# Four graph-attention layers on one core: layer 3's features turned through DRAM, layer 1's unit kept one higher, adj's turned copy in three places

## The chip, the cores and the metric

The kernel runs on one core of one Trainium2 chip. The metric is device time in microseconds (us), as the median of several executions. One further execution was taken with the hardware profiler; its views are what is read here. The engines are TensorE (PE in the profile, its weight loads PEld), VectorE (DVE), ScalarE (ACT), GpSimd (POOL) and SyncE (SP), which issues nearly all DMAs.

## The reference

128 graphs of 128 nodes with 512 float32 features go through four layers. Each layer normalises its input, applies relu and adds the result of an attention to the input. `adj` is an integer matrix per graph that says which nodes may attend to which.

```python
for layer in (L0, L1, L2, L3):
    x = x + layer(maximum(layernorm(x), 0))
# L1: two GAT layers; the first with 4 heads of 256 features
h = elu(gat_layer(x, mask, W1, ..., b1, concat=True))     # 1024 features
h = gat_layer(h, mask, W2, ..., b2, concat=False)         # 512 features
# L3: 8 heads of 64 features
xp = x @ W_proj;  out = relu(softmax(mask(leaky_relu(src_i + dst_j + b))) @ xp)
```

Layer 1's mask is indexed the other way round from the others (its softmax runs over the other axis), which is why the kernel holds `adj` turned as well.

## The kernel before, in words

One graph is one tile `xt` of 128 nodes x 512 features; everything of a graph stays in SBUF but for a few exchanges through DRAM. Up to 16 graphs are in flight (`FLYING`, line 22).

**Who sets the order.** The kernel is written as generators that yield single steps (`Step`, an instruction, or `Group`, several on one engine), requests for a tile (`Take`), or waits for another stream. A `Scheduler` (its `issue`, `rank`, `plan`) runs all of them against a small table of costs (`Step.estimate`) when the program is built, and so writes one fixed order for each engine. On the chip each engine takes its instructions strictly in that order and waits by semaphores. All steps are called from one line of `issue`, so that the profile puts nearly everything on line 331 (332 in the changed kernel); the tiles' names tell the steps apart. `plan` sets due times from one rehearsed graph, stretched over `FLYING` graphs.

**Tiles.** Kinds of tiles share pools of places: "mid" tiles (`h`, `ht`, `t`, `e1`, `et1`, `x2`, `x3`) have 18 together, "big" and "small" 10 and 22, each kind with a limit of its own. `adj` and its turned copy `at_t` have six places each (`FLYING // 4 + 2`, four graphs a tile).

**A layer.** `norm_relu` takes statistics on VectorE, three small steps on GpSimd and a relu on ScalarE (`h`). Where a layer multiplies features by a weight (layers 1 and 3), `transposed` turns `h` first: four 128x128 transposes on TensorE against `ident` into a PSUM bank, and a ScalarE copy to `ht`. `projected` multiplies `ht` with the weight: `w1x` in three parts of 344 columns for layer 1, `wpx` in two parts of 264 for layer 3. In the profile each float32 matmul stands as two records.

**Turning through DRAM.** VectorE's transpose turns squares of 32x32 in place; it doesn't move a square to another group of partitions. `exchanged` does the rest: four DMAs write a tile to DRAM square by square and one reads it back with rows and columns of squares exchanged. Layer 1's attention weights (512 columns, `et1`) and layer 3's (1024 columns, `et3`) are turned in this manner, layers 0, 1 and 2 use `dealt_out` for a single 128x128 tile. The last five graphs (`late`, `LATE = 5`) turn on TensorE instead, and the first eight in layer 0, the first three in layer 1.

**Layer 1's unit** (in `layer1`, after the first attention): per half of the 1024 features, VectorE adds `b1` to the PSUM bank into `y`, clamps `y` at 0 from above into `t`, ScalarE takes `exp(t)`, and VectorE makes `max(t - 1, y)`. `projected` then multiplies `y` with `w2x` (two parts of 257 columns, eight matmuls each) and VectorE adds `b2`. The weights' extra two columns of `w2x` are made once in `fold_w2`.

**adj turned.** `load_turned` reads four graphs of `adj` with squares exchanged, and VectorE turns the squares in place once per four graphs; `layer1`'s mask is made from it.

Of the kernel before, what the change touches and what calls it, by code (L numbers as in the profile page):

```python
# [9 lines left out]
F32 = mybir.dt.float32  # L10
I32 = mybir.dt.int32
# [7 lines left out]
LOWEST = -3.0e38  # L19
SLOPE = 0.2  # L20
EPS = 1e-5
FLYING = 16
PATIENCE = .3
LANES = 8
AHEAD = 1
# [4 lines left out]
SLOW = 0.7  # L30
FIRST = 0.8
MARGIN = .6
BIG, MID, SMALL = 10, 18, 22
SHARED = {k: ("big", BIG) for k in ("xl", "y1", "e3", "et3")}
SHARED.update({k: ("small", SMALL) for k in ("m0", "m1", "m2", "m3", "row", "e0", "et0")})
SHARED.update({k: ("mid", MID) for k in ("h", "ht", "t", "e1", "et1", "x2", "x3")})

# [90 lines left out]
class Take:  # L130


    def __init__(self, pool, shape, kind, most):
        self.pool, self.shape, self.kind, self.most = pool, shape, kind, most
        self.tag, self.bufs = SHARED.get(kind, (kind, most))


# [34 lines left out]
class Scheduler:  # L172
# [61 lines left out]
    def take(self, want):  # L234

        _, free = heapq.heappop(self.returned[want.tag])
        t = want.pool.tile(want.shape, F32, tag=want.tag, name=want.kind, bufs=want.bufs)
        self.tag_of[t.tensor.name] = want.tag, want.kind
        self.held[want.kind] = self.held.get(want.kind, 0) + 1
        return t, free  # L240
# [119 lines left out]
def kernel(  # L360
# [64 lines left out]
    products = const.tile([P, D], F32, name="products")  # L425
    minus_half = const.tile([P, 1], F32, name="minus_half")
    nc.gpsimd.memset(minus_half, -0.5)

# [26 lines left out]
    def few(to, values):  # L457
        with nc.allow_non_contiguous_dma(reason="at most 1024 values, once"):
            nc.scalar.dma_start(out=to, in_=values)

    def setup():
        for i, a in enumerate((l0_a1, l0_a2)):
            few(a0[:, :, i], a.rearrange("(c p) o -> p (c o)", p=P))
        for i, a in enumerate((l1_src1, l1_dst1)):
            few(a1[:, :, i], a.rearrange("h (c p) -> p (h c)", p=P))
        few(b1, l1_b1.rearrange("(c p) -> p c", p=P))

        w0 = []
        for c in range(KC):
            if c % 2 == 0:  # L470
                pair = yield tile_of("e3", 4, H3 * P)
                pair = pair.rearrange("p (c f) -> p c f", c=2)
            w0.append(pair[:, c % 2])
            yield S.dma_start(out=w0[c], in_=l0_w[c * P : (c + 1) * P])
        yield Fork(fold_u(w0))
        yield from load(0)
        yield from load_turned(0)
        for c in range(KC):
            yield S.dma_start(out=w1x[c][:, E1:], in_=l1_w1[c * P : (c + 1) * P])
        yield Fork(fold_w1())  # L480
        yield Fork(setup_second(), SECOND)

    def setup_second():
        yield from load(1)
        yield from load(2)
        vecs = []
        for row in (l1_src2, l1_dst2):
            vecs.append((yield tile_of("x2", 3, E2 + D))[:, :D])
            yield S.dma_start(out=vecs[-1], in_=row[0].partition_broadcast(P))
        for c in range(FC):  # L490
            yield S.dma_start(out=w2x[c][:, E2:], in_=l1_w2[c * P : (c + 1) * P])
        yield Fork(fold_w2(vecs), FOLD2)
        yield S.dma_start(out=b2[:, E2:], in_=l1_b2.partition_broadcast(P))
        yield Fork(setup_third(), THIRD)

    def setup_third():
# [64 lines left out]
    def fold_w2(vecs):  # L561
        for w in w2x:
            for s, vec in enumerate(vecs):
                yield from dot(w[:, E2:], vec, w[:, s : s + 1])
        give_back(*vecs)
        sched.reached.add("w2")

    def fold_w3(wa):
# [12 lines left out]
        sched.reached.add("wp")  # L581


    def norm_relu(xt):

        n = nc.vector.BN_STATS_DIM
        st = yield tile_of("st", 6, n + 5)
        yield V.bn_stats(st[:, :n], xt)
        mean, var = st[:, n : n + 1], st[:, n + 1 : n + 2]
        yield V.bn_aggr(st[:, n : n + 2], st[:, :n])  # L590
        ve, rstd, nmr = (st[:, i : i + 1] for i in range(n + 2, n + 5))
        yield G.tensor_scalar(ve, var, EPS, None, ALU.add)
        yield G.tensor_tensor(out=rstd, in0=ve, in1=minus_half, op=ALU.pow)
        yield G.tensor_scalar(nmr, mean, rstd, -1.0, ALU.mult, ALU.mult)
        h = yield tile_of("h", 5, D)
        yield A.activation(out=h, in_=xt, func=AF.Relu, bias=nmr, scale=rstd)
        give_back(st)
        return h

    def dot(h, vec, to):  # L600

        yield V.tensor_tensor_reduce(
            out=products,
            in0=h,
            in1=vec,
            scale=1.0,
            scalar=0.0,
            op0=ALU.mult,
            op1=ALU.add,
            accum_out=to,  # L610
        )

    def blocks_of(t):

# [223 lines left out]
    def layer1(xt, mask, late, near):  # L838
# [43 lines left out]
        for g in range(0, FC, 4):  # L882
            po = yield bank()
            yield Group(
                [
                    T.matmul(
                        po[:, (c - g) * P : (c - g + 1) * P],
                        lhsT=xl[:, c * P : (c + 1) * P],
                        rhs=et[c * P // F1],
                        start=True,  # L890
                        stop=True,
                    )
                    for c in range(g, g + 4)
                ]
            )
            if g + 4 == FC:
                give_back(fx, et[0])
            yg = y[:, g : g + 4, :]
            yield V.tensor_tensor(
                yg,  # L900
                po.rearrange("p (j q) -> p j q", q=P),
                b1[:, g : g + 4].unsqueeze(2).to_broadcast([P, 4, P]),
                ALU.add,
            )
            give_back(po)

            yg = yg.rearrange("p c q -> p (c q)")
            t = yield tile_of("t", 5, 4 * P)
            yield V.tensor_scalar(t, yg, 0.0, None, ALU.min)
            yield A.activation(out=t, in_=t, func=AF.Exp)  # L910
            yield V.scalar_tensor_tensor(yg, t, -1.0, yg, ALU.add, ALU.max)
            give_back(t)
        yield Until("w2")
        gx = yield tile_of("x2", 3, E2 + D)
# [19 lines left out]

    def layer3(xt, mask, late):

        h = yield from norm_relu(xt)
        ht = yield from transposed(blocks_of(h), "ht", 4)
        give_back(h)
        yield Until("wp")  # L940

        fx = yield tile_of("x3", 4, H3, E3 + K3 + 1)
# [102 lines left out]
    def load(b):  # L1045

        xs[b] = xpool.tile([P, D], F32, tag="xt", name="xt")
        yield S.dma_start(out=xs[b], in_=x[b])
        if b % AG == 0:
            adjs[b // AG] = adjp.tile([P, AG, P], I32, tag="at", name="at")  # L1050
            yield S.dma_start(
                out=adjs[b // AG], in_=adj[b : b + AG].rearrange("g i j -> i g j")
            )
            if b >= FLYING + AHEAD:
                yield Fork(load_turned(b))
            elif b:
                yield from load_turned(b)
        sched.reached.add(("x", b))

    def load_turned(b):  # L1060

        adjs_t[b // AG] = t = adjp.tile([P, AG, P], I32, tag="at_t", name="at_t")
        yield Group(
            [
                S.dma_start(
                    out=t[m * Q : (m + 1) * Q].rearrange("b g (r c) -> b (g r) c", r=R),
                    in_=adj[b : b + AG, :, m * Q : (m + 1) * Q].rearrange(
                        "g (r b) c -> b (g r) c", r=R
                    ),
                )  # L1070
                for m in range(R)
            ]
        )
        sched.reached.add(("loaded", b // AG))
# [6 lines left out]
    def graph(b):  # L1081
# [12 lines left out]
            yield V.transpose(flat, flat)  # L1094
            sched.reached.add(("turned", b // AG))
        yield Until(("turned", b // AG))
        at = adjs_t[b // AG][:, b % AG, :]
        m1 = yield tile_of("m1", 8, P)
        yield V.scalar_tensor_tensor(m1, at, 0.0, neg_off_diag, ALU.is_le, ALU.mult)
        yield from layer1(xt, m1, late, b < NEAR)  # L1100
        give_back(m1)
        m2 = yield tile_of("m2", 5, P)
# [5 lines left out]
        yield from layer3(xt, m3, late)  # L1108
        yield S.dma_start(out=out[b], in_=xt)

    adjs, adjs_t, xs = {}, {}, {}
    with tc.manual_schedule():
        usual = EARLY if EARLY % AG == 0 and EARLY < B - LATE else 0
        sched.rehearse(load(usual))
        sched.rehearse(load_turned(usual))
        sched.plan(sched.rehearse(graph(usual)))
        sched.reached.clear()
        sched.add(setup(), 0)
        flying, started = [], 0
        while True:  # L1120
            flying = [s for s in flying if not s.over]
            if started < B and len(flying) < FLYING:
                flying.append(sched.add(graph(started), started, "graph"))
                started += 1
            if not sched.issue() and started == B:
                break
# [49 lines left out]
```

## Time and profile before

| what | value |
|---|---|
| median of 3 runs | 3185.19 us (3175.77 to 3188.9) |
| profiled execution, its own time | 3175.9 us |
| its span, first to last instruction | 3174.1 us, 64620 instructions |
| mean granted TensorE clock | 0.993 |
| DMA: bytes, share of 16 engines (SP's queue) | 456.53 MB, 56.0% |
| DMAs that SP issues | 3614 |
| TensorE, records of `wpx,ht` | 2048, 505.1 us busy |
| TensorE, records of `w2x,y` | 4096, 967.5 us busy |
| VectorE, `y<-t,y` 128x512 | 256, 173.3 us busy, 677 ns each |
| ScalarE, `t<-t` 128x512 | 256, 160.4 us busy, 626 ns each |
| ScalarE, `h<-xt,st` 128x512 | 512, 412.2 us busy, 808 ns each |

How it is read: a group's line gives line, engine and operation, `out<-in` by the program's names, shapes, xcount, then busy time of the whole group, mean ns of one, and the idle time of the engine before its instructions with what ended most of it. A busy time is a union of spans, so overlapped instructions count once there but in full in the mean. The timeline gives start, duration, engine, operation and count, neighbours merged. The waits add up for each engine who released it. In the chain of waits, each piece is what the last instruction was waiting for, followed back to the start.

### The profile page before, as it was taken

The numbers are of one execution on the slowest core, as the hardware profiler recorded it, in microseconds if no ns is written. First come the engines' busy times: TensorE is split into PE (matmuls) and PEld (weight loads), VectorE is DVE, ScalarE is ACT, GpSimd is POOL, SyncE is SP. The second block draws the span as 40 slices with busy tenths as digits, with TensorE's granted clock in tenths as the row PEclk, the third lists the DMA queues.
The fourth block names the chain that finished last, engine by engine and source line by source line (L and its number), as shares of the span: only waits on it lengthen the run. The fifth ranks groups of instructions, "written<-read, shape, count | busy, mean of one in ns | idle before, by whom it ended". The sixth has DMA issues, their size and how long they took to land.

```text
span 3174.1 us, 64620 instructions
## 1 busy us (share of the span) xinstructions
PE 3133.4 (99%) x17434; PEld 2391.5 (75%) x17434; DVE 2869.5 (90%) x11663; ACT 2458.1 (77%) x7224; POOL 934.8 (29%) x2313
## 2 busy tenths in 40 slices
PE   8999999999999999999999999999999999999997
PEld 5777777777777777777777777777777777777786
DVE  6989989999999999999999999999999999899886
ACT  5777778778777877777787787778778777877867
POOL 2222222233232323323322332332323233233222
PEclk8999999999999999999999999999999999999998
DMA  7245565656565555555565556566565556555442
GB/s 193 53 96 144 152 155 150 150 148 160 147 154 153 153 148 156 155 146 154 147 160 148 153 159 149 146 154 152 153 158 151 147 155 161 145 147 147 114 112 82
DMA packets 770101, 460.68 MB, mean 145 GB/s; under 512 B 344776, under 2 KB 702408, under 8 KB 769736
## 3 DMA queue, kind: packets, MB, share of 16 engines
q1 hardware_dynamic: 765560, 456.53, 56.0%
q8 instruction: 140, 2.29, 0.3%
q14 instruction: 225, 1.84, 0.2%
q10 hardware_dynamic: 4176, 0.02, 0.1%
HBM read 299.00 MB, written 157.33 MB: 144 GB/s over the span
## 4 chain that ended last, share of the span: by engine, by line
PE 84%; DVE 6%; DMA 5%; ACT 2%; issue 1%; SPq 1%; POOL 1%; ACTq 0%; DVEq 0%; POOLq 0%
PE bank L331 84%; DVE e L331 2%; DMA et<-exchanged 1%; DMA row<-d 1%; DMA d<-r 1%; DVE st L331 1%; DMA et<-dealt 1%; DVE xt L331 1%; DVE products L331 1%; ACT e L331 1%; SPq L331 1%; DVE t L331 1%; POOL st L331 1%; DVE y L331 0%; DVE c L331 0%
## 5 line engine op out<-in xcount | busy, mean ns | idle before, releaser
L331 PE MATMUL bank<-w2x,y 128*128 128x257 f32 x4096 | 967.5, 381 | 0.0
L331 PE MATMUL bank<-w1x,ht 128*128 128x344 f32 x3072 | 951.6, 453 | 2.6 <-ACT ht L331 2.6
L331 PEld LDWEIGHTS bank<-w2x,y 128*128 128x128 f32 x4096 | 759.1, 190 | 138.6 <-issue 25.4
L331 PEld LDWEIGHTS bank<-w1x,ht 128*128 128x128 f32 x3072 | 573.3, 190 | 282.9 <-issue 27.3
L331 ACT ACTIVATE e<-e,f 128x128 f32<-128x128 f32 x2176 | 752.1, 391 | 8.4 <-DVE c L331 7.6
L331 POOL TENSOR_SCALAR st<-st 128x1 f32<-128x1 f32 x1024 | 343.5, 336 | 1174.6 <-DVE st L331 773.1
L331 ACT ACTIVATE e<-e,c 128x128 f32<-128x128 f32 x1408 | 535.4, 394 | 124.9 <-DVE e L331 78.5
L331 PE MATMUL bank<-wpx,ht 128*128 128x264 f32 x2048 | 505.1, 390 | 0.2 <-ACT ht L331 0.2
L331 ACT ACTIVATE h<-xt,st 128x512 f32<-128x512 f32 x512 | 412.2, 808 | 66.1 <-POOL st L331 61.6
L331 PEld LDWEIGHTS bank<-wpx,ht 128*128 128x128 f32 x2048 | 379.2, 191 | 81.0 <-issue 14.9
L331 POOL TENSOR_TENSOR st<-st,minus_half 128x1 f32<-128x1 f32 x512 | 353.8, 692 | 37.4 <-POOL st L331 0.2
L331 DVE BATCH_NORM_STATS2 st<-xt 128x6 f32<-128x512 f32 x512 | 346.4, 678 | 0.0
L331 DVE CUSTOM_DVE_ANT_0 e<-e,m 128x128 f32<-128x128 f32 x1484 | 334.4, 284 | 13.2 <-DMA e<-d 13.0
L331 PEld LDWEIGHTS bank<-et,xl 128*128 128x128 f32 x2048 | 267.1, 191 | 46.6 <-issue 16.9
L331 ACT COPY xl<-bank 128x344 f32<-128x344 f32 x384 | 168.0, 439 | 138.8 <-PE bank L331 134.7
L331 PE MATMUL bank<-h,et 128*128 128x512 f32 x512 | 265.8, 601 | 7.0 <-DMA et<-dealt 4.3
L331 PE MATMUL bank<-et,xl 128*128 128x128 f32 x2048 | 270.2, 275 | 1.6 <-DMA et<-exchanged 1.5
L331 DVE SCALAR_TENSOR_TENSOR xt<-bank,c,xt 128x512 f32<-128x512 f32 x256 | 190.6, 747 | 58.9 <-PE bank L331 55.4
L331 ACT ACTIVATE t<-t 128x512 f32<-128x512 f32 x256 | 160.4, 626 | 84.6 <-DVE t L331 83.0
L331 DVE TENSOR_TENSOR y<-bank,b 128x512 f32<-128x512 f32 x256 | 173.8, 679 | 24.1 <-PE bank L331 22.4
L331 ACT COPY ht<-bank 128x512 f32<-128x512 f32 x274 | 158.6, 580 | 38.0 <-PE bank L331 35.1
L331 DVE STREAM_TRANSPOSE e<-e 128x128 f32<-128x128 f32 (+1 forms) x481 | 187.8, 392 | 0.0
(85 smaller groups left out, 4220.2 us busy)
## 6 DMA issues: line engine op xcount, KB each, us to landing
e<-d SPq DMA_DIRECT2D x123, 512.0 KB
exchanged<-e SPq DMA_DIRECT2D x492, 128.0 KB
et<-exchanged SPq DMA_DIRECT2D x123, 512.0 KB
xt<-in_x_dram SPq DMA_DIRECT2D x128, 256.0 KB
out_dram<-xt SPq DMA_DIRECT2D x128, 256.0 KB
e<-d SPq DMA_DIRECT2D x125, 256.0 KB
exchanged<-e SPq DMA_DIRECT2D x480, 64.0 KB
et<-exchanged SPq DMA_DIRECT2D x120, 256.0 KB
```

The lines of the kernel that those rows point to most:

```text
L331: method(*args, **kw)
```

## The change

- **Layer 3** (all graphs but the last five): `norm_relu` writes `h` with its 32-column squares in another order (`dealt=True`), `exchanged` sends it through DRAM into a new "mid" tile `hs`, and one VectorE transpose of 128x512 turns the squares back into `h`, whose four blocks of 128 columns then take the place of `ht`. TensorE's four transposes and ScalarE's copy are gone there.
- **Layer 1**: `b1` is made one higher once, so that `y` holds the value plus 1; ScalarE takes `exp(y - 1)` straight from `y`, VectorE makes `max(min(t, 1), y)`. So `y` is the unit plus 1, without the clamp. `fold_w2` makes up for it: GpSimd sums the eight tiles of `w2x`, two matmuls with a tile of ones add that over the partitions, and VectorE subtracts it from `b2`.
- **adj**: `at_t` has three places, asked for from the scheduler and given back after the mask of the fourth graph; its load is a stream of its own from the 13th graph on.
- `FLYING` goes from 16 to 17, "mid" from 18 to 20 places, `h` may hold 6 of them (5 before).

```diff
-FLYING = 16
+FLYING = 17
...
-BIG, MID, SMALL = 10, 18, 22
+BIG, MID, SMALL = 10, 20, 22
+TURNED = 3
...
+        yield G.tensor_scalar(b1, b1, 1.0, None, ALU.add)
...
+        total = yield tile_of("x2", 3, E2 + D)
+        yield G.tensor_tensor(total, w2x[0], w2x[1], ALU.add)
+        for w in w2x[2:]:
+            yield G.tensor_tensor(total, total, w, ALU.add)
+        for to, part in zip(columns(b2, 2), columns(total, 2)):
+            pm = yield bank()
+            pm = pm[:, : to.shape[1]]
+            yield T.matmul(pm, lhsT=one.to_broadcast([P, P]), rhs=part, start=True, stop=True)
+            yield V.tensor_tensor(to, to, pm, ALU.subtract)
+            give_back(pm)
+        give_back(total)
...
-        h = yield tile_of("h", 5, D)
-        yield A.activation(out=h, in_=xt, func=AF.Relu, bias=nmr, scale=rstd)
+        h = yield tile_of("h", 6, D)
+        to, of = h, xt
+        if dealt:
+            to = h.rearrange("p (m c b) -> p c m b", c=KC, b=Q)
+            of = xt.rearrange("p (c m b) -> p c m b", c=KC, b=Q)
+        yield A.activation(out=to, in_=of, func=AF.Relu, bias=nmr, scale=rstd)
...
+    def features_turned(xt, turned_here):
+
+        if turned_here:
+            h = yield from norm_relu(xt)
+            ht = yield from transposed(blocks_of(h), "ht", 4)
+            give_back(h)
+            return ht
+        h = yield from norm_relu(xt, dealt=True)
+        to = yield from exchanged(h, "hs", 2)
+        yield V.transpose(
+            h.rearrange("p (c r b) -> p r c b", c=KC, b=Q),
+            to.rearrange("p (r c b) -> p r c b", c=KC, b=Q),
+        )
+        give_back(to)
+        return blocks_of(h)
...
-            yield V.tensor_scalar(t, yg, 0.0, None, ALU.min)
-            yield A.activation(out=t, in_=t, func=AF.Exp)
-            yield V.scalar_tensor_tensor(yg, t, -1.0, yg, ALU.add, ALU.max)
+            yield A.activation(out=t, in_=yg, func=AF.Exp, bias=minus_one)
+            yield V.scalar_tensor_tensor(yg, t, 1.0, yg, ALU.min, ALU.max)
...
-        h = yield from norm_relu(xt)
-        ht = yield from transposed(blocks_of(h), "ht", 4)
-        give_back(h)
+        ht = yield from features_turned(xt, late)
...
-            if b >= FLYING + AHEAD:
+            if b >= TURNED * AG:
                 yield Fork(load_turned(b))
...
-        adjs_t[b // AG] = t = adjp.tile([P, AG, P], I32, tag="at_t", name="at_t")
+        adjs_t[b // AG] = t = yield Take(work, [P, AG, P], "at_t", TURNED, I32)
...
+        uses[b // AG] = uses.get(b // AG, 0) + 1
+        if uses[b // AG] == AG:
+            give_back(at)
```

More of the change, by code (lines that the diff above doesn't have):

```diff
@@ L32 @@
 MARGIN = .6
-BIG, MID, SMALL = 10, 18, 22
+BIG, MID, SMALL = 10, 20, 22
+TURNED = 3
 SHARED = {k: ("big", BIG) for k in ("xl", "y1", "e3", "et3")}
 SHARED.update({k: ("small", SMALL) for k in ("m0", "m1", "m2", "m3", "row", "e0", "et0")})
-SHARED.update({k: ("mid", MID) for k in ("h", "ht", "t", "e1", "et1", "x2", "x3")})
+SHARED.update({k: ("mid", MID) for k in ("h", "ht", "t", "e1", "et1", "x2", "x3", "hs")})
 def size(ap):
@@ L130, with __init__ @@
 class Take:
-    def __init__(self, pool, shape, kind, most):
-        self.pool, self.shape, self.kind, self.most = pool, shape, kind, most
+    def __init__(self, pool, shape, kind, most, dtype=F32):
+        self.pool, self.shape, self.kind, self.most, self.dtype = pool, shape, kind, most, dtype
         self.tag, self.bufs = SHARED.get(kind, (kind, most))
@@ L236, in take @@
         _, free = heapq.heappop(self.returned[want.tag])
-        t = want.pool.tile(want.shape, F32, tag=want.tag, name=want.kind, bufs=want.bufs)
+        t = want.pool.tile(want.shape, want.dtype, tag=want.tag, name=want.kind, bufs=want.bufs)
         self.tag_of[t.tensor.name] = want.tag, want.kind
@@ L427 @@
     nc.gpsimd.memset(minus_half, -0.5)
+    one = const.tile([P, 1], F32, name="one")
+    nc.gpsimd.memset(one, 1.0)
+    minus_one = const.tile([P, 1], F32, name="minus_one")
+    nc.gpsimd.memset(minus_one, -1.0)
     E1, E2, E3 = 2 * H1, 2, 2
@@ L491, in setup_second @@
             yield S.dma_start(out=w2x[c][:, E2:], in_=l1_w2[c * P : (c + 1) * P])
+        yield S.dma_start(out=b2[:, E2:], in_=l1_b2.partition_broadcast(P))
         yield Fork(fold_w2(vecs), FOLD2)
-        yield S.dma_start(out=b2[:, E2:], in_=l1_b2.partition_broadcast(P))
         yield Fork(setup_third(), THIRD)
@@ L581, in fold_w3, with norm_relu @@
         sched.reached.add("wp")
-    def norm_relu(xt):
+    def norm_relu(xt, dealt=False):
         n = nc.vector.BN_STATS_DIM
@@ L1096, in graph @@
         yield Until(("turned", b // AG))
-        at = adjs_t[b // AG][:, b % AG, :]
+        at = adjs_t[b // AG]
         m1 = yield tile_of("m1", 8, P)
-        yield V.scalar_tensor_tensor(m1, at, 0.0, neg_off_diag, ALU.is_le, ALU.mult)
+        yield V.scalar_tensor_tensor(
+            m1, at[:, b % AG, :], 0.0, neg_off_diag, ALU.is_le, ALU.mult
+        )
+        uses[b // AG] = uses.get(b // AG, 0) + 1
+        if uses[b // AG] == AG:
+            give_back(at)
         yield from layer1(xt, m1, late, b < NEAR)
@@ L1109, in graph @@
         yield S.dma_start(out=out[b], in_=xt)
-    adjs, adjs_t, xs = {}, {}, {}
+    adjs, adjs_t, xs, uses = {}, {}, {}, {}
     with tc.manual_schedule():
@@ L1117 @@
         sched.reached.clear()
+        give_back(adjs_t[usual // AG])
+        uses.clear()
         sched.add(setup(), 0)
```

## The prediction

> **What bounds the kernel now.** I read the page's first part, then the three stretches of the run, then TensorE's timeline in the middle of it.
>
> The page says that TensorE is busy 99% of the span and VectorE 90%; the windows say where the rest lies.
>
> ```profile
> PE 3133.4 (99%) x17434; PEld 2391.5 (75%) x17434; DVE 2869.5 (90%) x11663; ACT 2458.1 (77%) x7224; POOL 934.8 (29%) x2313
> ```
>
> ```profile
> 100.00:3100.00 3000.00, 2987.41 (x16616) 2286.57 (x16615) 2752.66 (x11214) 2346.30 (x6904) 898.17 (x2216) 1.00 0.57 146
> 3100.00:3174.20 74.20, 57.39 (x464) 43.80 (x462) 45.66 (x210) 54.44 (x170) 14.44 (x46) 0.86 0.27 83
> 0.00:100.00 100.00, 88.57 (x358) 61.08 (x359) 71.15 (x241) 57.32 (x151) 22.23 (x51) 0.88 0.61 159
> ```
>
> Columns: stretch, length, then busy time of PE, PEld, DVE, ACT, POOL, the granted clock, the DMA share and GB/s. Between 100 and 3100 us PE is busy 2987 of 3000, at a granted clock of 1.00, DVE 2753 (91.8%) and ACT 78%. So the middle belongs to PE; only head and tail (some 30 us of idle PE) belong to chains. The chain that ended last agrees: 84% of it is PE. Since ends of matmuls are modelled, I look at starts:
>
> ```profile
> 1509.56 1.94 PE L331 MATMUL bank<-wpx,ht 128*128 128x264 f32 x8
> 1511.34 1.02 PE L331 MATMUL bank<-x,et 128*128 128x512 f32 x2
> 1512.20 0.60 PE L331 MATMUL bank<-ident,h 128*128 128x128 f32 x4
> 1512.64 2.48 PE L331 MATMUL bank<-w1x,ht 128*128 128x344 f32 x8
> 1514.95 0.60 PE L331 MATMUL bank<-ident,h 128*128 128x128 f32 x4
> 1515.39 1.90 PE L331 MATMUL bank<-w2x,y 128*128 128x257 f32 x8
> ```
>
> Each group starts when the one before has issued, with no gap: eight 344-column records take 2.31 us from start to start, four transposes of h 0.44 us both times (1512.20 to 1512.64, 1514.95 to 1515.39). Whatever leaves PE's queue in the middle shortens the run by its start-to-start time, as long as the others keep up.
>
> A rule of the Trainium skill would say otherwise: Perfetto Trace Analysis, "Identifying the Most-Contended Engine", calls matmul busy time a bad measure and asks for the weight loads' share. That is 75% here, and by it a quarter of PE would be free and the change worth nothing on PE. The starts in the trace decide against that here.
>
> **The change, part by part.**
>
> *Layer 3's turning.* Of 128 graphs, 123 (all but the last five) lose four PE transposes and one ACT copy of the result, and get four DMA writes, one read and one VectorE transpose.
>
> ```profile
> L331 PE MATMUL bank<-ident,h 128*128 128x128 f32 x1024 | 153.7, 274 | 4.3 <-ACT h L331 4.2
> L331 ACT COPY ht<-bank 128x512 f32<-128x512 f32 x274 | 158.6, 580 | 38.0 <-PE bank L331 35.1 <-DMA exchanged<-e 0.2
> L331 DVE STREAM_TRANSPOSE e<-e 128x512 f32<-128x512 f32 x120 | 82.6, 688 | 0.0
> L331 DVE TENSOR_SCALAR t<-y 128x512 f32<-128x512 f32 x256 | 105.9, 414 | 1.5 <-PE bank L331 0.7
> ```
>
> PE: 1024 records are eight per graph, half of them layer 3's. One lasts 274 ns, but they overlap: the price is 0.44 us a group, so 123 x 0.44 = **54 us less**, all of it on the path.
>
> The skill's TensorE: Matmul & The Clock Gate, "Part 4: PE-mode transpose", gives some 275 ns for one transpose inside a kernel, which the 274 ns agree with; charged four times it would make 123 x 1.1 = 135 us, two and a half times what the starts allow. VectorE: DVE Perf Modes, "Rules for kernel authors", also speaks against the change: a 128x128 transpose belongs on TensorE if PSUM will do as its target. It weighs one operation; here TensorE is the full engine.
>
> ACT: 123 x 0.580 = 71 us less, beside PE. The write of h in another order of 32-column blocks I cost at nothing: ACT's e operations take 391 ns over 32-column blocks and in one piece alike. DVE: 123 x 0.688 = 85 us more, by the row of the same size above; half of the 1229 ns of layer 3's 128x1024 transpose would give 76.
>
> SP: 615 more issues on 3614. Four such writes took 1.90 us in its timeline and a read 0.32 to 0.45, so some 2.3 us per graph or 280 us; SP's issuing goes from about 3614 x 0.43 = 1550 us to 1830, 59% of the new time. DMA: 256 KB out and in per graph, 64 MB on 457, so its share goes from 56% to about 65%.
>
> Latency: writes 1.9 us, landing 4.5, the read 5 to 7, the transpose 0.7, against 0.44 + 0.58 and their waits before: 11 to 13 us longer per graph. The landings are those that the chain of waits shows for the exchanges that the kernel already has:
>
> ```profile
> 2731.43 4.50 DMA exchanged<-e
> ```
> ```profile
> 835.14 5.42 DMA et<-exchanged
> 2097.35 7.12 DMA et<-exchanged
> ```
>
> What hides it is that 17 graphs are in flight instead of 16. A graph stays 16 x 24.8 = 397 us now (24.8 us is 3174 / 128) and 17 x 24.4 = 415 us then: 18 us more, for 13 needed. Without that cover PE would wait at layer 3's projection. New waits and who stands behind: SP's read of hs waits for its four writes, and all of SP's later DMAs stand behind it; VectorE's transpose waits for the read, with all of VectorE behind it; PE's wpx matmuls wait for that. In the new order of SP, a median of 8 places lie between the last write and the read (fewest 3), or 8 x 0.46 = 3.7 us of issuing, so most reads are issued when the writes have landed. Such reads now stop DVE little: 10.6 us in all before `e<-et`. For the new ones I allow between 0 and 0.3 us a graph on PE (0 to 37 us) and take 0, since PE's waits for such transfers now are 1.5 us (`et<-exchanged`) and 4.3 us (`et<-dealt`) in the whole run.
>
> *Layer 1's unit one higher.* 256 VectorE clamps go: 256 x 0.414 = 106 us. ScalarE's exponential gets a bias per partition: the 128x512 row without one lasts 626 ns, those with one scale from PSUM 651 and 682, the one with both 808. That is +6 to +14 us by the nearest, 0 to 47 at the ends; I take 10. The other VectorE step keeps its shape (677 ns). So DVE: 85 - 106 + 1 = **20 us less** (30 by the lower price), ACT: 71 - 10 = 61 less. Neither is on the path; but DVE's share of the middle stays just below PE's: 2753 - 20 on 2950 is 92.6%. The clamp was also a step between a matmul and the next one, so this path gets shorter by 0.4 us twice a graph; I count nothing for it.
>
> *The correction of b2.* Once, after the 16 products of w2x (they end at 61.6 us): seven POOL sums of 128x514, two 257-column matmuls (four records, 0.9 us from eight in 1.73), two VectorE subtractions. No row has such a sum: the nearest is POOL's 128x128 at 626 ns, from below; stretched in proportion, with two operands, 5 us at most. Seven are 4 to 35 us; I take 1.7 us each (its slope over 128x1, 276 ns, carried to 514 columns), 12 us. First use of w2x is at 89.9 us now, so they end in time; but three norms (POOL at 64 to 73 us) stand behind them. That costs 0 to 12 us of a head in which PE idles 11; I take 3.
>
> GPSIMD Engine Reference, "Elementwise", gives 2.6 cycles per element at 1.2 GHz for two inputs: an estimate of 1.1 us each, 8 in all, and no other sum.
>
> *adj's three places.* Nothing. A turned group is needed from its load until the fourth graph's mask in layer 1, about (4 + 17/4) x 24.4 = 200 us, and three places last 3 x 4 x 24.4 = 293 us. If that cover went, the load would be issued later; the plan holds that stream back, not SP's queue.
>
> **Sum.** PE: -54 + 1 + 3 = -50 us against the profiled execution's 3175.9 us: 3126. That execution is 9 us under the median of the runs shown (3185.2; from 3175.8), so against the median: **3135 us**.
>
> **Rivals.**
> 1. *VectorE or new waits eat half.* For it: DVE 92.6% in the middle, every step in a fixed order, and 37 us as the upper bound above. Against it: DVE loses 20 us itself, and its largest wait for a DMA is 22.4 us over the run (`row<-d`). 3185 - 13 to -30: 3155 to 3172.
> 2. *The DMA queue becomes the bound, slower than before.* SP issues in order, and its DMAs take eight completion semaphores in turn. From issue to landing they take 3.7 us on average (worked out from the trace's issues and landings): 1.14 per us keep 4.2 in flight. With 1.36 per us it is 5.0, and 5.8 if landings stretch with the DMA share. If bursts reach eight, SP stands, the exchanges come late and PE waits at layer 3. To lose, PE must wait 50 + 16 us, from about 0.55 us on in each of the 123 graphs; at 0.7 it is 3185 - 50 + 86 = 3221. Against it: 5.8 is not 8, and the added flight.
> 3. *No gain, because the transposes were hidden* (the weight-load view): 3185. The starts speak against it.
> 4. *More than the sum*, if PE's present waits shrink with the lighter ACT and shorter layer 1: 3100 to 3115.
>
> **Chances.** Forecast (3115 to 3155) 0.66, rival 4 0.07, rival 1 0.13 (0.11 of it faster by over 0.5%, which is about what a measurement of this kernel tells from no change: under 3169), rival 3 0.06, rival 2 0.08. Faster 0.84, same 0.08, slower 0.08. For the range I leave out the slowest case and the outer halves: 3103 to 3172.
>
> **What would show it.** Right: 532 `ident,h` records instead of 1024, starts still without gaps, PE near 99.5% of the middle, DVE about 2850 us, ACT 2397, DMA near 65%. Wrong: PE idle before `wpx` with `DVE h` as releaser, DVE waiting for `hs`, SP waiting on DMAs far above the 118 us of its largest such wait (`d<-r`), or PE idle between 60 and 90 us. The forecast fails if PE's busy time in the middle falls by less than 40 us per 123 graphs, or if its idle time grows by more than 20.

## The result and the profile after

The changed kernel takes 3295.19 us (median of 4 runs, 3291.03 to 3300.1), the one before 3181.65 us in the same comparison (3175.77 to 3188.9). The ratio is 1.0356 [1.0327, 1.0386]: slower by 3.6%, where 3135 us was forecast. The profiled execution took 3291.03 us, its span is 3289.2 us.

First the page: busy times of the engines, and SP's DMA queue (packets, MB, share of 16 engines).

```profile
PE 3126.5 (95%) x16946; PEld 2358.7 (72%) x16946; DVE 2846.1 (87%) x11532; ACT 2409.9 (73%) x7101; POOL 934.6 (28%) x2323
...
q1 hardware_dynamic: 854120, 521.05, 60.1%
```

Then the three stretches of the run, with the columns of the windows shown before.

```profile
0.00:100.00 100.00, 85.08 (x326) 57.46 (x327) 70.96 (x231) 51.54 (x131) 30.82 (x61) 0.85 0.56 155
100.00:3200.00 3100.00, 2969.56 (x16047) 2247.33 (x16046) 2715.04 (x11041) 2293.51 (x6771) 882.69 (x2200) 0.99 0.61 162
3200.00:3289.20 89.20, 71.83 (x576) 53.87 (x574) 60.12 (x262) 64.82 (x201) 21.05 (x62) 0.87 0.36 101
```

488 matmul records are gone, DVE's sum fell by 23 us and ACT's by 48, and yet no engine is fuller: in the middle PE fell from 99.6% to 95.8% busy, DVE to 87.6%, and DMA stands at 61%. Head and tail leave PE idle for 15 and 17 us, 11 and 17 before. So the time went into gaps in the middle that nobody fills. The groups tell in front of which work they lie (after the bar: idle time before the group, and what ended it). Before:

```profile
L331 PE MATMUL bank<-et,xl 128*128 128x128 f32 x2048 | 270.2, 275 | 1.6 <-DMA et<-exchanged 1.5
...
L331 PE MATMUL bank<-x,e 128*64 128x65 f32 x3936 | 143.5, 226 | 3.0 <-DVE e L331 3.0
```

After, with the groups that the prediction named:

```profile
L332 PE MATMUL bank<-et,xl 128*128 128x128 f32 x2048 | 279.6, 280 | 43.4 <-DMA et<-exchanged 41.2 <-ACT e L332 1.8
...
L332 ACT ACTIVATE t<-y,minus_one 128x512 f32<-128x512 f32 x256 | 183.4, 717 | 71.3 <-DVE y L332 70.0
...
L332 PE MATMUL bank<-x,e 128*64 128x65 f32 x3936 | 144.8, 227 | 48.9 <-DVE e L332 39.8 <-issue 2.7 <-ACT e L332 2.1
...
L332 DVE STREAM_TRANSPOSE h<-hs 128x512 f32<-128x512 f32 x123 | 85.5, 695 | 8.8 <-DMA hs<-exchanged 8.0 <-issue 0.6
L332 PE MATMUL bank<-ident,h 128*128 128x128 f32 x532 | 82.6, 279 | 12.8 <-ACT h L332 12.5
```

The new transfer itself is hardly waited for (`hs<-exchanged`, 8.0 us). What comes late are transfers that were there before: the attention weights of layer 1 (`et,xl`) and of layer 3, which `x,e` needs. The waits say it of DVE too (us in total, times, longest), and the last lines are SP's own largest waits for DMAs. Before:

```profile
DVE e L331 <- DMA row<-d: 22.4, 35, 1.8
...
DVE e L331 <- DMA et<-exchanged: 10.6, 9, 3.0
...
SPq L331 <- DMA d<-r: 118.4, 110, 4.2
```

After:

```profile
DVE e L332 <- DMA row<-d: 76.9, 88, 3.4
...
DVE e L332 <- DMA et<-exchanged: 51.7, 25, 6.2
...
SPq L332 <- DMA e<-d: 102.9, 78, 3.9
SPq L332 <- DMA d<-r: 55.8, 54, 3.0
```

SP itself does not stand longer for DMAs: over all its rows these waits sum to 330 us before and 270 us after.

**One gap, followed back.** PE's timeline shows it idle for 3.69 us before layer 3's products (in brackets: idle before, and the releaser):

```profile
2006.98 2.00 PE L332 MATMUL bank<-x,e 128*64 128x65 f32 x32 [3.69 <-DVE e L332]
```

DVE's timeline: the transpose that makes this `e` stood 4.84 us for its transfer, with all of DVE behind it.

```profile
2005.59 1.25 DVE L332 STREAM_TRANSPOSE e<-et 128x1024 f32<-128x1024 f32 x1 [4.84 <-DMA et<-exchanged]
```

SP's timeline: the read `et<-exchanged` was issued at 1994.17 (the first of the two in its row), behind ten DMAs in 5.4 us, and the chain of waits gives it 11.39 us from issue to landing, where the two reads shown of before took 5.42 and 7.12.

```profile
1988.82 0.38 SPq L332 DMA_DIRECT2D d<-r  x1
1989.26 2.15 SPq L332 DMA_DIRECT2D exchanged<-e  x4
1991.77 0.81 SPq L332 DMA_DIRECT2D row<-d  x2
1992.69 0.41 SPq L332 DMA_DIRECT2D e<-d  x1
1993.16 0.50 SPq L332 DMA_DIRECT2D row<-d  x1
1993.70 0.42 SPq L332 DMA_DIRECT2D e<-d  x1
1994.17 3.77 SPq L332 DMA_DIRECT2D et<-exchanged  x2
1997.98 4.79 SPq L332 DMA_DIRECT2D exchanged<-h  x4
```
```profile
1994.17 11.39 DMA et<-exchanged
```

Right behind it four writes of the new exchange take 4.79 us to issue instead of 1.9. Each of SP's DMAs counts on one of eight completion semaphores in turn (some 530 on each in this run, 452 before), and waits there for the DMA eight places back. That is not what holds these four. By the trace's semaphore events the first stood for ScalarE's `h` (until 1998.99), and the second took 1.90 us although the last DMA on its semaphore had been done since 1994.76. What is unusual here is the load: from 1998 to 2006 us the 16 DMA engines are busy for 0.93 of the time (0.61 in the middle). So this one gap looks like a burst of transfers; e7 below shows that bytes are not what the run's loss hangs on.

**A gap costs twice.** PE's timeline elsewhere in this run:

```profile
934.69 1.59 PE L332 MATMUL bank<-x,e 128*64 128x65 f32 x32 [3.76 <-DVE e L332]
936.21 3.76 PE L332 MATMUL bank<-w1x,ht 128*128 128x344 f32 x8
939.81 1.05 PE L332 MATMUL bank<-et,xl 128*128 128x128 f32 x8
```

After the 3.76 us gap eight 344-column records take 3.60 us from start to start (936.21 to 939.81) instead of 2.31: the granted clock is 0.5 for a step of 3.41 us. Between 200 and 3000 us such steps make 51 us in this run, none before; at half the clock about 25 us of work are lost in them (an estimate). PE's gaps in that stretch are 129.8 us, 12.6 before.

### The profile page after: what moved, and what is told of

The parts are those of the page before. It is cut to its first block, busy times and chain, and to the rows that moved or that the text cites. A ratio compares the mean times of both kernels' runs of the same rounds, so it can differ in the third digit from the quotient of the medians.

```text
span 3289.2 us, 64325 instructions
## 1 busy us (share of the span) xinstructions
PE 3126.5 (95%) x16946; PEld 2358.7 (72%) x16946; DVE 2846.1 (87%) x11532; ACT 2409.9 (73%) x7101; POOL 934.6 (28%) x2323
## 5 line engine op out<-in xcount | busy, mean ns | idle before, releaser
L332 POOL TENSOR_SCALAR st<-st 128x1 f32<-128x1 f32 x1024 | 368.9, 363 | 978.9 <-DVE st L332 780.0
L332 PE MATMUL bank<-wpx,h 128*128 128x264 f32 x1968 | 482.4, 388 | 3.0 <-DVE c L332 1.2
L332 PEld LDWEIGHTS bank<-wpx,h 128*128 128x128 f32 x1968 | 369.7, 190 | 86.3 <-issue 15.1
L332 POOL TENSOR_TENSOR st<-st,minus_half 128x1 f32<-128x1 f32 x512 | 315.3, 619 | 30.7
L332 PE MATMUL bank<-et,xl 128*128 128x128 f32 x2048 | 279.6, 280 | 43.4 <-DMA et<-exchanged 41.2
L332 PE MATMUL bank<-h,et 128*128 128x512 f32 x512 | 257.1, 605 | 9.3 <-DMA et<-dealt 6.7
L332 ACT ACTIVATE t<-y,minus_one 128x512 f32<-128x512 f32 x256 | 183.4, 717 | 71.3 <-DVE y L332 70.0
L332 DVE STREAM_TRANSPOSE e<-et 128x1024 f32<-128x1024 f32 x123 | 152.4, 1239 | 76.1 <-DMA et<-exchanged 51.7
L332 POOL TENSOR_SCALAR m<-m 128x128 f32<-128x128 f32 x128 | 76.3, 596 | 466.0 <-DVE m L332 344.0
L332 DVE CUSTOM_DVE_ANT_1 e<-row,m 128x128 f32<-128x128 f32 x361 | 134.1, 383 | 80.1 <-DMA row<-d 76.7
```

The source lines that it names most:

```text
L332: method(*args, **kw)
```

## The experiments

My theory after the result: the sums on PE, DVE and ACT hold, and the five added DMAs a graph make other DMAs late. Rivals: bytes on the DMA engines; SP's issuing; the order that the planner writes around the DMAs; the changes beside the turning (unit, places, 17 graphs); the latency of the new turn itself. Ratios are to the kernel before, on the same chip.

**Without the exchange's DMAs** (all else of the change stays):

```diff
-        to = yield from exchanged(h, "hs", 2)
-        yield V.transpose(h squares, to squares)
+        to = yield tile_of("hs", 2, D)
+        yield V.transpose(to squares, h squares)
```

> The changed kernel without the exchange through DRAM: layer 3's features go through the VectorE transpose of 128x512 into hs and straight to TensorE, so their blocks of 32 are not exchanged and layer 3's result is not the reference's. All else of the change stays (places, 17 graphs, layer 1's unit, adj's three places). Theory A (the five added DMAs per graph make the other transfers and SP's queue late): the 50 us of the prediction show up, 3120 to 3145 us. Theory B (the new fixed order, with 17 graphs and adj's three places, is worse by itself): near the changed kernel, 3250 to 3300. Theory C (VectorE's added transposes): as B, since they are all still there.

Measured: 3135.04 us, 0.984 [0.9812, 0.9869].

```profile
100.00:3050.00 2950.00, 2933.13 (x16066) 2238.69 (x16064) 2713.28 (x11045) 2315.33 (x6783) 845.60 (x2201) 1.00 0.58 148
```

PE is at 99.4% of the middle, with DVE at 92.0%, as forecast. The whole loss, 3295 - 3135 = 160 us or 1.3 us a graph, goes with the five DMAs: with them on the chip, or with their places in the order.

**The turning alone, and all but the turning:**

```diff
 # e2: before, with features_turned, "hs" and h's six places; 16 graphs
 # e3: after, with
-        ht = yield from features_turned(xt, late)
+        ht = yield from features_turned(xt, True)
```

> The kernel before with layer 3's turning through DRAM alone: 16 graphs, 18 mid places, the clamp in layer 1 and adj's six places stay. Theory A: as slow as the changed kernel or slower, 3270 to 3350 us, since all 615 DMAs are there and one graph less is in flight. Theory B: 3120 to 3150, the gain without the loss. Theory C: slower than the changed kernel by some 0.8 us a graph, 3350 to 3400, since VectorE's clamp stays as well.

> The changed kernel with layer 3 turned on TensorE as before: 17 graphs, 20 mid places, layer 1's unit one higher, adj's three places. Theory A: as the kernel before or up to 30 us faster, 3150 to 3190 us. Theory B: slower than the changed kernel or about as slow, 3280 to 3350. Theory C: as A.

Measured: 3283.54 us, 1.0306 [1.0261, 1.0351], and 3187.66 us, 1.0013 [1.0002, 1.0025]. Unit, places of `adj` and the 17th graph together move next to nothing (0.1%), and the 17th graph does not cover the turning: with it 3295, without it 3284, with intervals that overlap.

**The same five DMAs, used by nobody**, beside the kernel before, which goes on turning on TensorE; and the same with 16 columns instead of 512 (8 KB in place of 256 KB each way):

```diff
-        give_back(h)
+        yield Fork(beside(h))   # exchanged(h, "hs", 2), then give_back
 # e7:  exchanged(h[:, : 4 * R], "hs", 2)
```

> The kernel before, with layer 3's features turned on TensorE as ever, and beside that the same four writes and one read of h per graph through DRAM, into a tile that nothing reads; no engine waits for them but SP and the places that they hold. Theory A: the transfers alone cost what the changed kernel lost, 3260 to 3340 us (about 3181 + 113 + 50 if all of it comes from the load and SP's order). Theory B and C: 3180 to 3200.

> The kernel before with the five unused DMAs per graph of the run that added them, but with 16 columns of h instead of 512, so 8 KB instead of 256 KB out and in, with as many pieces to write. Theory A1: as with the full size, 3270 to 3320 us. Theory A2 by bytes: 3185 to 3205.

Measured: 3309.66 us, 1.0388 [1.0358, 1.0418], and 3310.75 us, 1.0367 [1.0337, 1.0397]. No engine's work waits for these transfers, so the loss does not need the latency of the turn; a thirty-second of the bytes costs the same, so it does not need the bytes either.

**Another queue for the exchange: ScalarE's, then GpSimd's:**

```diff
-        to = yield from exchanged(h, "hs", 2)
+        to = yield from exchanged(h, "hs", 2, A)   # e5;  G in e9
-        self.lanes = {"SP": [Transfer()] * LANES, "POOL": [Transfer()] * LANES}
+        self.lanes = {k: [Transfer()] * LANES for k in ("SP", "POOL", "ACT")}   # e5 alone
```

The second line gives ScalarE eight places of its own in the plan; GpSimd has them already. So in both runs the order is planned as if SP were as free as before the change.

> The changed kernel with the five DMAs of layer 3's turning issued by ScalarE's queue instead of SP's; the bytes, the packets and the order's table stay. Theory A1 (SP's queue: one in-order queue that is too full): the loss goes, 3130 to 3190 us, with ScalarE some 280 us busier at issuing. Theory A2 (the load on the 16 DMA engines makes all transfers late): 3270 to 3310, as the changed kernel.

> The changed kernel with the five DMAs of layer 3's turning issued by GpSimd's queue, whose completions are counted on semaphores of its own (SP's and ScalarE's DMAs share the eight of the trace, 100 to 107, as the run on ScalarE's queue showed). Theory L (the eight shared completion semaphores: a DMA waits until the eighth before it has landed): the loss goes, 3125 to 3180 us, unless GpSimd's norm steps become late. Theory M (the number of pieces or DMAs on the 16 engines, whoever issues them): 3270 to 3310. Theory O (the fixed order, planned with SP too full): the plan changes too, 3130 to 3180.

Measured: 3299.7 us, 1.0333 [1.0245, 1.042], and 3228.44 us, 1.014 [1.0064, 1.0216]. In the trace ScalarE's DMAs count on the same eight semaphores as SP's (100 to 107), GpSimd's on others (111 to 118). Here the semaphores do show on the chip: in e5 SP stands 789 us for DMAs instead of 270, and 117.9 of them for `exchanged<-h`, writes that ScalarE issues and whose data SP does not need. ScalarE's queue gains nothing, GpSimd's takes back 67 us. (ScalarE itself stood for `exchanged<-h` in e5, 37.4 us of it before its `e`, so that run is not clean by itself.) The Trainium skill, DMA: Bandwidth & Descriptors, "Issuing engines are not separate DMA queues", says that issuing from several engines saves only issuing time. e5 gained not even that; whether e9's 67 us are issuing time, own semaphores or the freer plan, no run here tells apart. The rest of e9's loss against 3135 was not found: GpSimd there issues 615 DMAs of about 0.6 us each beside its small steps, and DVE still waits 84.4 us for `row<-d`.

**Fewer DMAs, one write and one read** through `dealt_out`, on SP's queue and on GpSimd's:

```diff
+        yield V.transpose(hs "p (m n c) -> p m c n", h squares)
+        to = yield from dealt_out(hs, "hu", 4)      # e10: ..., G)
+        return [to "p (n c) -> p c n"[:, c] for c in range(KC)]
```

> The changed kernel with layer 3's features turned by one write and one read instead of four and one: VectorE's transpose comes ahead of the DMAs and the 128 partitions are dealt out, as the kernel does for 128x128 tiles. The same 256 KB go out and in; SP issues 246 more than before instead of 615. Theory A1: the loss against the 50 us gain (some 160 us) shrinks with the number of issues, to 246/615 of it or less: 3135 to 3200 us. Theory A2: 3270 to 3300, for the bytes are the same.

> The turning by one write and one read, both issued by GpSimd's queue: 246 DMAs on semaphores of their own, SP's number as before the change. Theories L and O: 3125 to 3165 us, the best of all so far. Theory M: 3200 to 3220, as with two DMAs on SP.

Measured: 3215.63 us, 1.007 [1.0037, 1.0104], and 3231.03 us, 1.0148 [1.008, 1.0217]. Both carry a price of their own: TensorE's weights now lie four elements apart, and their load takes 322 ns instead of 190. The row of after, then that of e6:

```profile
L332 PEld LDWEIGHTS bank<-wpx,h 128*128 128x128 f32 x1968 | 369.7, 190 | 86.3 <-issue 15.1 <-PE bank L332 2.7 <-DVE m L332 1.0
```
```profile
L332 PEld LDWEIGHTS bank<-wpx,hu 128*128 128x128 f32 x1968 | 484.8, 322 | 42.1 <-issue 14.6 <-DVE e L332 4.0 <-DVE r L332 2.6
```

The `wpx` records then start 234 ns apart instead of 223 (the medians): 1968 x 11 ns = 22 us. Without that e6 would stand at some 3194 (an estimate): three DMAs fewer take back some 100 of 160 us, and some 59 us over e1 stay. 30 of these are longer gaps of PE (47.3 us against 16.9 between 200 and 3000 us); the rest is not placed (ScalarE's write of `h` also takes 932 ns there, 808 before).

**Four small pieces instead of squares**, unused, beside the kernel before:

```diff
+            [S.dma_start(out=d[r : r + 1], in_=h[r * Q : r * Q + 1]) for r in range(R)]
+        yield S.dma_start(out=to[:R], in_=d)
```

> The kernel before with five unused DMAs per graph again, but of four pieces of 2 KB written and four read in all, instead of 512 and 128: nearly no bytes and no pieces. Theories L and O, which count DMAs: 3260 to 3320 us, as with 8 KB in 512 pieces. Theory M by pieces: 3185 to 3210.

Measured: 3234.19 us, 1.0158 [1.0109, 1.0207], less than half of e7's loss with as many DMAs. The planner also charges such a write less (0.35 us of issuing, not 0.5), so pieces and plan are not told apart here.

**Is it the chip or the order?** The order is fixed when the program is built, by a planner that keeps eight DMAs under way at most (`LANES`). Two kernels keep the order and issue none of the exchange's DMAs:

```diff
+            if isinstance(want, Step):
+                want.calls = []        # e12 on e4; e13 on after, whose
+                                       # transpose then reads a constant
```

> The fixed order of the run with five unused DMAs per graph, but without issuing them: every engine has the instructions of that order, SP 615 fewer. The result is the reference's. Theory O (the loss lies in the order as it was planned around the added DMAs): 3270 to 3320 us. Theories L and M (the loss lies in the DMAs on the chip): 3180 to 3215.

> The order of the changed kernel, instruction for instruction, but the 615 DMAs of layer 3's turning are not issued and VectorE's transpose reads a constant tile instead, so layer 3's result is not the reference's. Against the run without the exchange (3135 us), only the order differs; against the changed kernel (3295), only the DMAs. Theory O (the loss of 160 us lies mostly in the order): 3240 to 3295 us. Theory L (it lies mostly in waits for the eight shared semaphores and late landings on the chip): 3135 to 3190. The first pair of such runs gave the order 83 of 125 us, which here would be some 106: 3240.

Measured: 3264.66 us, 1.0254 [1.0215, 1.0293], and 3266.03 us, 1.0251 [1.0182, 1.032]. So 83 of e4's 125 us, and 131 of after's 160 (3266 - 3135), come with the order alone. The two executions of e13 lie 16 us apart, so its part is 123 to 139 us. The middle and the first late wait of e13:

```profile
100.00:3100.00 3000.00, 2898.17 (x15582) 2194.03 (x15582) 2650.05 (x10809) 2242.16 (x6631) 867.85 (x2155) 0.99 0.56 143
```
```profile
PE bank L332 <- DMA et<-exchanged: 33.9, 25, 3.5
```

The DMA share is back at 0.56, and PE still stands 102 us, in front of the same work (41.2 us of that wait in after).

**The planner's table**, with the instructions unchanged: landings planned 1 us later, and 0.5 us of SP's time charged for each DMA, on the changed kernel; no limit of eight on the changed kernel; a limit of six on the kernel before.

```diff
-MARGIN = .6
+MARGIN = 1.6      # e8, and 0.5 us of issuing for each DMA
-LANES = 8
+LANES = 64        # e14, on after
+LANES = 6         # e16, on before
```

> The changed kernel with another table behind its fixed order: every DMA issue costs 0.5 us of SP (0.35 or 0.5 before), and every transfer is counted as landed 1 us later. No instruction is added or taken; only the order changes. Theory A3 (the loss is that the order was planned with issues and landings too short): 3130 to 3200 us. Theories A1 and A2 in their plain form (the queue or the engines are full whatever the order): 3260 to 3320.

> The changed kernel with one number of the plan's table changed: the plan lets 64 DMAs be under way on SP's queue instead of 8. The instructions are the same, the chip has its eight semaphores as before, only the order differs. If the plan loses by keeping to eight: 3140 to 3230 us. If the plan was right to keep to eight, so that SP's queue now stands more on the chip: 3290 to 3400.

> The kernel before with one number of the plan's table changed: the plan lets 6 DMAs be under way on SP's queue instead of 8. Same instructions, same chip, only the order differs. If an order planned around a full set of semaphores is slow by itself (theory O with the semaphores in the plan as the cause): 3210 to 3300 us. If not: 3175 to 3195.

Measured: 3520.13 us, 1.1023 [1.0991, 1.1055]; 3272.17 us, 1.0271 [1.0202, 1.0339]; 3316.26 us, 1.0409 [1.0372, 1.0446]. e16 is the plainest: the kernel before, not one DMA added, loses 129 us (3316.26 - 3187.42) when its planner believes in six places instead of eight. e8 was to repair the order and made it far worse. And leaving the limit out of the changed kernel's plan helps little, if at all (the intervals of e14 and after overlap): its waits move to other transfers, and SP stands 373 us for DMAs instead of 270.

```profile
DVE e L332 <- DMA row<-d: 130.7, 124, 4.5
...
PE bank L332 <- DMA et<-dealt: 91.4, 68, 4.7
```

**Paying with other DMAs.** If the number of DMAs makes the loss, the change should win once others go. A `row` (a column of scores spread over the partitions) costs a write and a read; TensorE can make it by one transpose into a PSUM bank:

```diff
-            rows = yield from row(other)
+            rows = yield bank()
+            yield T.transpose(rows[:, :P], other.to_broadcast([P, P]), ident)
 # e15: layers 0 and 2;  e17: layers 0, 1 (second) and 2;  e18: layer 0
```

> The changed kernel with the attention's row of layers 0 and 2 spread by one TensorE transpose into a PSUM bank (as the last five graphs do) instead of a VectorE transpose and two DMAs: 4 DMAs a graph fewer, so one more than before the change instead of five, and two transposes a graph more on TensorE, some 2 x 0.11 x 123 = 27 us. If the number of DMAs on SP makes the loss by the plan and the semaphores: 3150 to 3200 us, better than the kernel before or level. If it is something else in layer 3's turning: 3280 to 3320.

> As the run with the rows of layers 0 and 2 on TensorE, with layer 1's second row there too: one DMA a graph fewer than the kernel before, three transposes a graph more on TensorE (3 x 0.11 x 123 = 41 us against the 54 saved). If the order and the semaphores have room enough with one DMA a graph more (3157 us), this run only pays TensorE's 13 us more: 3160 to 3180. If room still lacked there, it is faster: 3135 to 3155.

> As the run with the rows of layers 0 and 2 on TensorE, but of layer 0 alone: three DMAs a graph more than the kernel before, one transpose a graph more. A loss that grows evenly with the DMAs gives about halfway between 3157 and 3295, 3200 to 3240 us; one that sets in only near five gives 3140 to 3170, the fastest of all.

Measured: e15 3156.77 us, 0.9913 [0.989, 0.9935]; e17 3160.67 us, 0.992 [0.990, 0.994]; e18 **3146.96 us, 0.9883 [0.9866, 0.9899]**, the fastest whole kernel, ahead of both. Its middle, and two of its rows:

```profile
100.00:3100.00 3000.00, 2978.14 (x16382) 2269.00 (x16380) 2730.61 (x11072) 2325.50 (x6852) 839.60 (x2240) 1.00 0.63 166
```
```profile
L332 PE MATMUL bank<-et,xl 128*128 128x128 f32 x2048 | 276.3, 278 | 0.1
...
L332 PE MATMUL bank<-x,e 128*64 128x65 f32 x3936 | 143.3, 226 | 2.5 <-DVE e L332 2.5
```

PE is back at 99.3% with the DMA engines *busier* than in the changed kernel (0.63 against 0.61), and both late groups wait no more. One transpose a graph (in the 115 graphs that used a `row` in layer 0) costs PE 115 x 0.11 = 13 us, so 3135 + 13 = 3148 leaves nothing for the remaining three added DMAs. In one table (mean under way: DMAs per us times mean time from issue to landing, and PE's gaps, both between 200 and 3000 us):

| kernel | DMAs a graph against before | mean under way | PE's gaps, us | time, us |
|---|---|---|---|---|
| before | 0 | 4.4 | 12.6 | 3181.7 |
| e16, six places in the plan | 0 | 4.3 | 108.7 | 3316.3 |
| e1, exchange left out | 0 | 4.2 | 16.9 | 3135.0 |
| e13, not issued, order of after | 0 | 4.7 | 101.7 | 3266.0 |
| e17 | -1 | 4.0 | 9.2 | 3160.7 |
| e15 | +1 | 4.6 | 14.2 | 3156.8 |
| e6 | +2 | 5.2 | 47.3 | 3215.6 |
| e18 | +3 | 5.0 | 17.5 | 3147.0 |
| e11 | +5 | 5.0 | 48.7 | 3234.2 |
| e4 | +5 | 5.1 | 112.0 | 3309.7 |
| e2 | +5 | 5.1 | 124.8 | 3283.5 |
| after | +5 | 5.4 | 129.8 | 3295.2 |

The loss is not in proportion to the DMAs: one and three more with a row taken away (e15, e18) cost nothing that shows, five cost some 150 us in e2 and after, and e6 with two more keeps its 59. Nor does the mean under way decide it: e16 and e13 have gaps of over 100 us at 4.3 and 4.7, e18 has none to speak of at 5.0, e11 has 48.7 at 5.0. e16 and e13 lose by their order, with no DMA added on the chip. A caution: taking a row away also removes a small VectorE transpose, a write and a read that something waits for, not only a number. The places of the tiles `h` and `hs` are no rival, for e15 and e18 keep them as they are in after.

## Why the prediction was wrong, step by step

- **PE: 54 us less.** Right. 532 `ident,h` records, as forecast, and e1 gave 3135 us, the forecast itself. So was the reading that the weight loads' 75% is no room: a quarter of PE idle would have made e1 equal to before.
- **DVE 20 us less**: 23. The new transpose takes 695 ns (688 used).
- **ACT 61 us less**: 48. The exponential with a bias takes 717 ns, 91 more than the 626 without, not 40; 256 x 0.091 = 23 us instead of 10. Off the path. The Trainium skill, ScalarE: Activation LUTs, "What ACT_TABLE_LOAD costs", gives some 93 ns for each such operand, which this agrees with and which I had not weighed.
- **b2's correction**: the POOL sums take 1.6 and 1.8 us (1.7 used). **adj, unit, 17 graphs at nothing**: right, by e3.
- **DMA share 65%**: 60%. In part the run got longer (over 3126 us the same busy time would be 63%), in part the packets took less time per byte than before; bytes were not the question (e7).
- **The new waits: here it failed.** "For the new ones I allow between 0 and 0.3 us a graph on PE (0 to 37 us) and take 0, since PE's waits for such transfers now are 1.5 us (`et<-exchanged`) and 4.3 us (`et<-dealt`) in the whole run." It cost 1.3 us a graph, 160 us in all (e1). The bound came from what the *existing* transfers cost in an order planned without the new ones. It priced the new transfer's own lateness, which is small (8.0 us), and not what five more DMAs do to the order that the planner writes for everything else: `et<-exchanged` went from 1.5 to 41.2 us before PE's products, and 131 of the 160 us are there even when the five are planned but not issued (e13). The cover I named, one more graph in flight, hides a longer path of one graph, not an order in which others' transfers come late (e2, without it, lost about as much). Of the waits that I named as signs of being wrong none came: PE idles 3.0 us before `wpx`, DVE 8.0 us for `hs`, and SP's largest wait for a DMA is 102.9 us, not far above 118. Only PE's idle time grew as named, by 117 us in the middle's gaps (12.6 to 129.8).
- **Rival 2 had the direction**, at 0.08 and with 3221 us; its price, 0.7 us a graph, is about half of what was measured. Its mechanism is SP that stands on the chip when bursts fill the eight semaphores. The changed kernel's trace does not show that: SP stands 270 us for DMAs, 330 before. So that it came near is in part luck. Its eight places do count, but in the plan: the kernel before loses 129 us when its planner believes in six (e16). My argument against it, "5.8 is not 8", looked at the mean on the chip, which became 5.4 and decides nothing (the table). I looked for the loss on the chip only, and most of it was in the order already: with five more DMAs to place the planner wrote an order in which other transfers, and what waits for them, come late (e13).

**What is shown and what is not.** Shown: with the five DMAs out of plan and chip 160 us are back (e1); neither bytes nor the turn's latency nor the other parts of the change are needed for such a loss (e7, e4, e3); the order alone makes most of it (e13); a smaller limit in the plan is enough to make one (e16); one row fewer undoes it (e18). Argued: that in the changed kernel's plan it is the eight places, and not the time that the planner charges SP for each DMA. e16 shows that places can; e11, with 0.35 us charged instead of 0.5, lost less than half of e7; e5 and e9 take both off SP's plan. Not shown: that the eight semaphores hold SP on the chip in the changed kernel. Open: how the order is spoiled step by step, what the 29 us are that come with issuing the DMAs (3295 - 3266), and the rest of the loss in e6 and with GpSimd's queue.

## What to carry to other kernels

When a change adds DMAs to a kernel whose order a planner fixes, the planner's own limits are part of the price: here the order alone took 131 of 160 us, with the DMAs not even issued, while neither bytes nor the mean number under way told which kernel would lose. Price the new work by what it does to everybody's place in the order, not by the waits that the present transfers show. Two kernels tell order from chip cheaply: the new order without the new instructions (e13), and the old instructions under a tighter limit in the plan (e16). An exchange that is worth its DMAs can be paid for with small ones: leaving out one small write and one read of 64 KB, which a TensorE transpose replaces, made a loss of 3.6% into a gain of 1.2%.

## What the runs showed of the hardware

- Two gaps of PE of about 3.7 us were followed by a step of 3.41 us at a granted clock of 0.5, in the middle of a busy run. The Trainium skill, TensorE: Matmul & The Clock Gate, "HAM oscillation — how this bites in real kernels", describes this for gaps over some 3.4 us. The trace agrees only in part: a gap of 3.71 us that ended at 1240.83 was followed by no such step, and some steps came after gaps of 1.9 to 2.4 us.
- SP's and ScalarE's DMAs shared eight completion semaphores (100 to 107), GpSimd's had their own (111 to 118). With the exchange on ScalarE's queue SP stood 117.9 us for ScalarE's writes (e5; 7.2 us for the same writes on its own queue).
- Weights four float32 elements apart loaded in 322 ns instead of 190, and this reached the matmuls' spacing (234 ns instead of 223).
- A per-partition bias added 91 ns to a 128x512 exponential.
- With the DMA engines at 63% of the middle nothing was lost (e18); with 56%, in an order planned for more DMAs, 131 us were (e13 against e1). Their share did not tell which kernel would lose.
